# Serial scatters, a later row lookup, router counts one slot on, and another form for the first magnitudes: four small moves in an attention and mixture-of-experts kernel

## The chip, the cores and the metric

The kernel runs on one core of a Trainium2 chip. The metric is the device time of one execution in microseconds (us), lower is better. The engines are PE (TensorE), DVE (VectorE), ACT (ScalarE), POOL (GpSimd) and SP (SyncE, which here only issues DMAs). Each engine takes its instructions in the order of the program; they wait for each other by semaphores. POOL issues the indirect DMAs, that is, scatters and gathers whose row numbers lie in SBUF.

## What is computed

The reference is one transformer layer on x of 8 batches x 1024 tokens x 512 features, in float32. The attention has 16 heads of 32. Its queries, keys and values are cosines and sines, looked up in a table, of the normalised input divided by 1 + |w|; the expert layer sends each token to two of eight experts, 160 places per batch and expert.

```python
x = x + attention(layernorm(x))     # theta_q = xh / (1.0 + jnp.abs(w_q)) + b_q + t * phi_q
...                                 # theta_o = out / (1.0 + jnp.abs(w_out)) + b_out
x = x + ffn(layernorm(x))
...
probs = jax.nn.softmax(x @ Wr + br, axis=-1)
topk_p, topk_e = jax.lax.top_k(probs, K)
pos_all = jnp.cumsum(oh, axis=1) - oh           # oh: one-hot of the chosen experts
keep = pos < cap
h = jax.nn.relu(jnp.einsum('enc,ech->enh', buf, W1) + b1[:, None, :])
y = jnp.einsum('enh,ehc->enc', h, W2) + b2[:, None, :]
```

## The kernel before

The order of the work on PE, ACT, DVE and SP is written out by hand: generators are advanced step by step, and the order in which Python calls them is the order in the queues.

**Start.** Input rows of the first batch are loaded tile by tile (L161). DVE takes statistics of the first two tiles (`first_stats`, L235, L236), prepares 1 / (1 + |w|) for values (`magnitude` and L240 on `rows_in`) and the biases (L242, `wrap`), then the same for queries and keys (`magnitude` and L257 on `inv_qk`), and then the statistics of the other six tiles (L235, L236), the inverse root (L361 to L369), and the normalisation, shared with ACT (L424 to L431). `magnitude` is called a third time for `inv_o` within the first slot. Meanwhile POOL fills constants, clears the value tiles (L377) and computes the position angles (L469), for which it needs `vecs` (L253). Then come transposes (L216), angles and their sines, and the DMAs that put queries and keys into place (L571).

**Attention slots.** A slot n is a batch b and a group c of four heads, n = 4b + c, 32 slots in all. Its two pairs of heads each take `scores` (PE L684 and L698 into a double PSUM bank of `ps_sc`, then ACT's exponential L704, ten tiles) and `attend` (L718, read by DVE L726). While one slot runs, the next one's queries and keys are prepared: `qk_pre` (transposes L216, DVE L525), `angle` (L438), squares, sines, and `qk_post` (DVE L448 and the DMAs L609). `turn` transposes the attention's result. `two_banks()` hands out one of three double banks; transposes, scores, and the router share them.

**Router.** The router of batch b - 1 is a generator advanced within the slots of batch b. In slot c = 1 it computes the logits, in c = 2 the choice of experts (`part`, up to the step named "places"). The next step counts the earlier tokens of each expert:

```python
yield "places"
place = one_bank()[:, : NTT * E]
flat = lambda t: t.rearrange("p t e -> p (t e)")
tokens_out(place, before, flat(mask), start=True, stop=False)
tokens_out(place, ones, flat(prior), start=False, stop=True)
```

`tokens_out` (L858) issues the small matmuls; DVE reads the bank twice (L966, L967), and the step ends at "slots". Before, `route_on(2)` takes this step in slot c = 2, between the first pair's `attend` and the second pair's `scores`. In slot c = 3 the generator ends: slots are computed, and `scatter` issues 16 indirect DMAs (L769) that write token numbers and gates into `slot_d[b]`. Scatters into one `slot_d[b]` wait for each other unless that is declared away; `together=True` declares it away. `late=True` and `together=True` both put the scatter behind POOL's share of the weight mixing (`mixed`, L1213) in POOL's queue. `fetch_slots` (L1005) reads the finished slots back into `meta` when all scatters of the batch have landed.

**Experts.** Weights are mixed by differences (Winograd's form of Strassen: seven products for eight). Each expert has two parts: rows of the first batches (768 rows; three blocks of layer two) and the rest (512 rows). `chunks` lists the 16 parts. Layer one runs over eight groups q (`Hidden`, products L1238, copies and activations on ACT L1248 to L1280, additions on DVE). During the first part's layer one, `ending` is advanced at each product: it finishes the last slot's output and routes the last batch. It ends with `fetch_slots(B - 2)`, the last batch's 16 scatters (`together=True`) and `fetch_slots(B - 1)`. W2 of the first expert (eight DMAs of 512 KB, L1056) is loaded at once, during that layer one.

Layer two of the first part is `layer2`, block by block: products L1352, ACT copies (L1364, L1375, L1377), DVE additions (L1369 to L1400), the gate on ACT (L1311), and an indirect DMA that adds the rows to the output (`send`, L1316). Each of its 21 steps advances `aside` once, which prepares the second part:

- `find_rows(1)` (DVE L1084) turns the slots of the second part into row numbers (`source`); it needs all slots of the last batch. Before, it stands between layer one and layer two.
- `gather(1)`, two steps into layer two (`behind(2, ...)`): four gathers on POOL (L1096), each put out to DRAM (SP L1107) and read back in quarters (SP L1113), a transpose on DVE (L1174) for each, then four additions (L1184 to L1187) that make the operands `xe` and `xe_s` of the second part's layer one.

The mixing of the second part's first weights (`mix_w1`, L1213) is called at the start of the last block.

Of the kernel before, what the change touches and what calls it, by code (L numbers as in the profile page):

```python
# [17 lines left out]
ALU = mybir.AluOpType  # L18
# [8 lines left out]
NTT = S // P  # L27
NCH = D // P
HPC = P // DH
E, HID, TOPK = 8, 2048, 2  # L30
# [30 lines left out]
UNITS = PER_RAD * FINE  # L61
# [13 lines left out]
def preln_attn_moe_kernel(  # L75
# [21 lines left out]
    nc = tc.nc  # L97
# [35 lines left out]
    own = to_router.pool("own", 1, **left)  # L133
# [12 lines left out]
    def token_tiles(dram_rows):  # L146
# [3 lines left out]
    rows_in, spare = (  # L150
        row2.tile([P, D], F32, name="xn2").rearrange("p (i f) -> p i f", f=NCH)[:, :n, :]
        for n in (3, 2)
    )
# [31 lines left out]
    t = xmp.tile([P, NTT, D], F32, name="x_mid").rearrange("p (i t) d -> p i (t d)", i=2)  # L185
    room = [t[:, i, :].rearrange("p (i s) -> p i s", i=2) for i in range(2)]
    for t in (base_first, room[0]):
        nc.gpsimd.iota(
            t, pattern=[[0, 2], [1, S]], base=0, channel_multiplier=0,
# [13 lines left out]
    inv_qk = own.tile([P, 2 * NCH], F32, name="inv_qk")  # L203
# [14 lines left out]
    def magnitude(t):  # L218

        nc.vector.scalar_tensor_tensor(t, t, -1.0, t, ALU.mult, ALU.max)  # L220
        nc.vector.tensor_scalar(t, t, 1.0, None, ALU.add)
        nc.vector.reciprocal(t, t)

    def wrap(t, spare):

        nc.vector.tensor_scalar(spare, t, ROUNDT, ROUNDT, ALU.add, ALU.subtract)
        nc.vector.tensor_tensor(t, t, spare, ALU.subtract)
# [9 lines left out]

    first_stats(0, 2)
    magnitude(rows_in[:, 0, :])
    nc.vector.tensor_scalar(rows_in[:, 0, :], rows_in[:, 0, :], UNITS, None, ALU.mult)  # L240
    b_rows = rows_in[:, 1:, :]
    nc.vector.tensor_scalar(b_rows, b_rows, UNITS, SUM_SHIFT * FINE, ALU.mult, ALU.add)  # L242
    wrap(b_rows, spare)
# [10 lines left out]

    nc.vector.tensor_copy(inv_qk, vecs[:, : 2 * NCH])
    magnitude(inv_qk)
    nc.vector.tensor_scalar(inv_qk, inv_qk, UNITS, None, ALU.mult)  # L257

    ones = own.tile([P, P], F32, name="ones")
    nc.gpsimd.memset(ones, 1.0)  # L260
# [501 lines left out]
    scattered = {b: [] for b in range(B)}  # L762
    mixed = []

    def scatter(count=2 * NTT * TOPK, together=False, late=False):

        for _ in range(min(count, len(scatters))):
            b, idx, src = scatters.pop(0)
            queued = nc.gpsimd.indirect_dma_start(  # L769
                out=slot_d[b], out_offset=bass.IndirectOffsetOnAxis(ap=idx, axis=0),  # L770
                in_=src, in_offset=None,
            )
            ins = queued.ins
            if together or late:
                tc.add_manual_dep(
                    ins, mixed[-1].name,
                    mybir.DependencyInfo(
                        mybir.DependencyClass.NoSync, mybir.DependencyReason.DATA
                    ),
                    reason="behind the mixture",  # L780
                )
            if together:
                for other in scattered[b]:
                    tc.declare_no_dep(ins, other, reason="rows of their own")
            scattered[b].append(ins)

    def router(b):
# [292 lines left out]
    def find_rows(i):  # L1080

        js = slice(chunks[i][1], chunks[i][1] + 2 * chunks[i][2])
        lo, hi = REACH[i]
        nc.vector.tensor_scalar(  # L1084
            source[:, :, js], meta[:, :, js, 0], float(hi * S), float(lo * S),
            ALU.min, ALU.subtract,
        )
# [102 lines left out]
    def behind(count, gen):  # L1190
        for _ in range(count):
            yield
        yield from gen

    def start(gen, box):
        for box[0] in gen:
            yield
# [303 lines left out]
    def seconds(i, hid):  # L1501

        free = places(i, hid)
        if chunks[i][2] == 2:
            rooms = [(free[6 * n : 6 * n + 3], free[6 * n + 3 : 6 * n + 6]) for n in range(2)]
            results = free[12:14]
        else:
            rooms = [(free[:4], free[4:7])] * 2
            results = free[7:9]
        return {w: Second(i, hid, w, *rooms[n % 2]) for n, w in enumerate((5, 2, 3, 4))}, results  # L1510
# [113 lines left out]
    def load_ahead(k):  # L1624
        if k < len(order_):
            load_w1(*order_[k])
# [3 lines left out]
    def experts_begin():  # L1630
# [6 lines left out]
        mix_w1(0, 0)  # L1637

    def experts(ending):
        pools["hp"] = to_end.pool("hp", 1, **right)  # L1640
        pools["ps_tr"] = to_end.pool("ps_tr", 2, space=PSUM, reuse_waits="tile")
        pools["ps_p"] = to_end.pool("ps_p", 6, space=PSUM, reuse_waits="tile")
        box = first_parts
        mixes = loads = iter(())
        for i, (e, j0, nh) in enumerate(chunks):
            parts, box = box[0], [None]
            hid = pools["hp"].tile([P, NHQ, 7, HALF], F32, name="hid")
            tiles, second, early_sums = None, None, iter(())
            if nh == 2:
                second = seconds(i, hid)  # L1650
                early_sums = itertools.chain(second[0][5].weights(), second[0][2].weights())
            ahead = rows_ahead(i + 1) if i and i + 1 < len(chunks) else iter(())
            for q in range(NHQ):
                if i or q != NHQ - AHEAD - 1:
                    load_ahead(i * NHQ + q + AHEAD)
                some(3, loads)
                if q + 1 < NHQ:
                    mix_w1(i, q + 1)
                if i and q > 1:
                    some(4 if q < 4 else 8, mixes)  # L1660
                next(ahead, None)
                if 2 < q < 7:
                    some(2, early_sums)
                beside = [ending] if i or q < NHQ - 2 else [mixes] * (q + 3 - NHQ)
                tiles = layer1(Hidden(i, q, parts, hid, beside), tiles, q == NHQ - 1)
                if i == 0 and q == NHQ // 2:
                    rest(ending)
                    to_router.close()
                    for name, bufs in (("w2p", 1), ("yp", 5), ("bp", 1)):
                        pools[name] = to_end.pool(name, bufs, reuse_waits="tile", **left)  # L1670
                    load_ahead(NHQ - 1)
                    load_b2(0)
                    rest(load_w2(0))
                    mixes = mix_w2(0)
            rest(mixes)
            if i == 0:
                find_rows(1)
            rest(ahead)
            aside = start(gather(i + 1), box) if i + 1 < len(chunks) else iter(())
            if i == 0:  # L1680

                aside = behind(2, aside)

            def mix_next():
                if i + 1 < len(chunks):
                    mix_w1(i + 1, 0)

            if i:
                extra = layer2_quad(
                    i, hid, second, aside, mix_next if nh == 2 else lambda: None  # L1690
                )
                if nh > 2:
                    some(2, aside)
                    for step in range(5):
                        if step == 4:
                            mix_next()
                        next(extra)
                        if step < 2:
                            some(2, aside)
            else:  # L1700
                for block in range(nh):
                    if block == nh - 1:
                        mix_next()
                    for _ in layer2(i, block, hid):
                        next(aside, None)
            rest(aside)
            if i % 2 and e + 1 < E:
                load_b2(e + 1)
                loads = load_w2(e + 1)
                mixes = mix_w2(e + 1)  # L1710
# [22 lines left out]
    begin = False  # L1733
    place, residual = [None], iter(())
    first_gather = gather(0)
    for n in range(NCK):
        more, late = n + 1 < NCK, last is not None
        b, c = divmod(n, NCH)
# [16 lines left out]
        def route_on(slot):  # L1755
            if c == slot and route is not None:
                next(route)
# [15 lines left out]
            turn(0, halves0, pos)  # L1773
        if more:
            angle(*qk_st)
        if begin:
            next(route)
        if n and n + 2 < NCK:
            load_base(n + 2)
# [80 lines left out]
            next(post)  # L1860
        some(NTT, *products)
        route_on(1)
        route_on(2)
        next_pairs = rest(post) if more else None

        es1, halves1 = [[], []], []
# [2 lines left out]
        begin = c == 0 and late  # L1869
# [25 lines left out]
    def ending():  # L1895

        o_st = o_pre(NCK - 1, pos_n)
        scatter(NTT * TOPK // 2, late=True)
        yield
        sine(o_st[1])  # L1900
        square(o_st[0])
        for _ in range(3):
            yield
        for _ in o_post(NCK - 1, o_st):
            yield
        yield
        steps = 0
        for name in router(B - 1):

            if steps in (0, 3):  # L1910
                scatter(NTT * TOPK // 4, late=True)
            steps += 1

            for _ in range({"tiles": 5, "places": 5}.get(name, 1)):
                yield
        fetch_slots(B - 2)
        scatter(together=True)
        fetch_slots(B - 1)

    experts(ending())  # L1920
# [31 lines left out]
```

## Time and profile before

| | us |
|---|---|
| median of 3 executions | 3180.25 (3177.90 to 3182.41) |
| the profiled execution | 3179.05 |
| its span, first to last instruction | 3177.3 |
| PE, DVE, ACT, POOL busy | 3096.0, 2310.1, 1676.5, 420.6 |
| mean granted clock of TensorE | 0.998 |
| start, to the first scores | 0 to 34.66 |
| attention slots | 34.66 to 1255 |
| first part: layer one, layer two | 1255 to 1343.7, to 1417.0 |
| the other 15 parts | 1417 to 3177 |

The profile gives for each instruction its start from the beginning of the span, its duration, its line in the kernel, and the tiles that it writes and reads ("out<-in"). In square brackets stands how long its engine was idle before it, and what ended that ("<-"). The list of waits adds these up: engine and line that waited, whom for, total, times, longest. "issue" means that the engine waited for nothing that the profile shows. The durations of POOL are rough.

### The profile page before, as it was taken

What the parts mean: (1) busy time and instruction counts of PE and PEld (TensorE: products, weight loads), DVE (VectorE), ACT (ScalarE), POOL (GpSimd) and SP (SyncE); (2) the same over time, 40 slices, a digit from 0 to 9 for tenths busy, and PEclk for the clock granted to TensorE, in tenths of its full rate; (3) what the DMA queues carried; (4) which work ended last, traced back from release to release, by engine and by line L of the source; (5) the groups of instructions that cost most, each with busy time, mean ns of one, the idle gap of its engine ahead of it and who ended that gap; (6) DMA issues with size and microseconds to landing.
All of it is one profiled execution on the core that took longest, in us unless ns stands there. A gap on an engine that the chain in (4) does not pass through costs nothing.

```text
span 3177.3 us, 52455 instructions
## 1 busy us (share of the span) xinstructions
PE 3096.0 (97%) x20086; PEld 2147.3 (68%) x20086; DVE 2310.1 (73%) x4808; ACT 1676.5 (53%) x2630; POOL 420.6 (13%) x387
## 2 busy tenths in 40 slices
PE   5999999999999999999999999999999999999998
PEld 2544454444444444589699699699698698698697
DVE  8888888888788776638668658758657667767765
ACT  7888888888788885413423423423423423423423
POOL 3000202020111122410110110110110110110010
PEclk9999999999999999999999999999999999999999
DMA  5435454554545352433523523523533433433421
GB/s 167 147 100 166 125 155 135 148 146 133 164 130 160 81 167 70 134 77 99 156 53 90 153 54 97 146 57 98 141 63 101 132 67 100 129 69 106 119 57 24
DMA packets 288554, 358.80 MB, mean 113 GB/s; under 512 B 28376, under 2 KB 199088, under 8 KB 276272
## 3 DMA queue, kind: packets, MB, share of 16 engines
q1 hardware_dynamic: 264944, 312.20, 33.3%
q0 software_dynamic: 22912, 43.22, 7.3%
q8 instruction: 160, 2.62, 0.4%
q14 instruction: 90, 0.74, 0.1%
q10 hardware_dynamic: 448, 0.02, 0.0%
HBM read 207.02 MB, written 81.22 MB: 91 GB/s over the span
## 4 chain that ended last, share of the span: by engine, by line
PE 78%; ACT 11%; DVE 7%; issue 2%; DMA 2%; SPq 0%; another core or an unknown queue 0%; POOLq 0%; POOL 0%; ACTq 0%; DVEq 0%
PE ps_p L1238 30%; PE ps_p L1474 10%; PE ps_p L1537 10%; PE ps_s L684 9%; PE av L718 9%; PE ps_p L1352 8%; ACT e L704 6%; PE ps_s L216 1%; ACT qk_c L594 1%; DMA xn_d<-xn 1%; ACT t_r L445 1%; ACT qk_r L445 1%; PE ps_s L698 1%; ACT L594 1%; DVE qk_f L525 1%
## 5 line engine op out<-in xcount | busy, mean ns | idle before, releaser
L684 PE MATMUL ps_s<-qk 64*128 64x512 f32 (+3 forms) x3072 | 584.1, 502 | 33.5 <-DMA qk<-qk_r 12.5
L704 ACT ACTIVATE e<-ps_s 128x1024 f32<-128x1024 f32 (+1 forms) x640 | 555.1, 944 | 85.6 <-PE ps_s L698 46.2
L718 PE MATMUL av<-e,v 128*64 128x512 f32 (+3 forms) x3072 | 509.5, 488 | 0.0
L684 PEld LDWEIGHTS ps_s<-qk 64*128 64x128 f32 x3072 | 261.4, 187 | 219.6 <-ACT e L704 93.1
L718 PEld LDWEIGHTS av<-e,v 128*64 128x64 f32 x3072 | 206.0, 137 | 278.8 <-issue 258.6
L1238 PE MATMUL ps_p<-xe,t 128*128 128x256 f32 (+1 forms) x1024 | 317.7, 433 | 2.7 <-ACT hid L1271 2.7
L1238 PE MATMUL ps_p<-xe_s,t 128*128 128x256 f32 (+1 forms) x1024 | 317.8, 433 | 2.3 <-issue 2.3
L1238 PE MATMUL ps_p<-xe,w 128*128 128x256 f32 (+1 forms) x1024 | 317.6, 433 | 0.0
L1316 POOL DMA_INDIRECT out_dram<-y,slots x80 | 127.4, 1593 | 1267.8 <-ACT y L1311 1016.9
L769 POOL DMA_INDIRECT slot_d<-token,slot x128 | 153.8, 1201 | 994.4 <-issue 636.4
L1238 PEld LDWEIGHTS ps_p<-xe_s,t 128*128 128x128 f32 x1024 | 194.3, 190 | 84.0 <-issue 3.7
L1238 PEld LDWEIGHTS ps_p<-xe,t 128*128 128x128 f32 x1024 | 194.2, 190 | 83.4 <-ACT hid L1271 3.3
L1238 PEld LDWEIGHTS ps_p<-xe,w 128*128 128x128 f32 x1024 | 193.7, 190 | 78.2
L1537 PE MATMUL ps_p<-w_t,hid 128*128 128x256 f32 x960 | 212.4, 379 | 0.8 <-DVE y L1590 0.8
L1281 DVE TENSOR_TENSOR hid<-hid 128x256 f32<-128x256 f32 (+1 forms) x128 | 63.0, 492 | 203.7 <-ACT hid L1279 200.9
L1537 PEld LDWEIGHTS ps_p<-w_t,hid 128*128 128x128 f32 x960 | 180.0, 190 | 24.4 <-DVE y L1590 1.2
L1238 PE MATMUL ps_p<-xe_s,w 128*128 128x256 f32 (+1 forms) x512 | 158.9, 433 | 1.1 <-ACT p L1254 1.1
L726 DVE TENSOR_SCALAR av_sb<-av,inv_o 128x512 f32<-128x512 f32 x128 | 94.8, 746 | 70.7 <-PE av L718 70.7
L1352 PE MATMUL ps_p<-w,hid 128*128 128x256 f32 x640 | 142.9, 379 | 0.0
L1474 PE MATMUL ps_p<-w,hid 128*128 128x128 f32 x1104 | 141.8, 275 | 0.0
L1311 ACT ACTIVATE y<-y,slots 128x256 f32<-128x256 f32 (+1 forms) x120 | 65.9, 578 | 142.8 <-DVE y L1389 105.5
L698 PEld LDWEIGHTS <-keys_b 64*128 64x128 bf16 x1536 | 78.9, 95 | 90.7 <-issue 71.9
(291 smaller groups left out, 5229.3 us busy)
## 6 DMA issues: line engine op xcount, KB each, us to landing
w<-in_L_ffn_W_dram SPq DMA_DIRECT2D x256, 256.0 KB
w<-in_L_ffn_W_dram SPq DMA_DIRECT2D x64, 512.0 KB
qk<-qk_c SPq DMA_DIRECT2D x124, 256.0 KB
qk<-qk_r SPq DMA_DIRECT2D x120, 256.0 KB
qk_base<-base_d SPq DMA_DIRECT2D x28, 1024.0 KB
xn_d<-xn SPq DMA_DIRECT2D x72, 256.0 KB
rows_d<-xg SPq DMA_DIRECT2D x70, 256.0 KB
x_mid<-in_L_attn_x_dram SPq DMA_DIRECT2D x16, 1024.0 KB
```

What stands on the lines that cost most here:

```text
L684: nc.tensor.matmul(ps[:, a, at : at + w], lhsT=pair[r, 1, kb * P : (kb + 1) * P], rhs=pair[r, 0, q0 : q0 + w], start=at == 0, stop=not own ...
L698: nc.tensor.matmul(out_, lhsT=keys_b[r, part, :], rhs=late, start=False, stop=part == 1, skip_group_check=True,)
L704: nc.scalar.activation(e, ps[:, :, :n], AF.Exp, scale=UNIT * UNIT / math.sqrt(2 * DH))
L718: nc.tensor.matmul(av[a * 64 : (a + 1) * 64, q0 - 512 * h :], lhsT=vt[:, kb, 2 * pr + a, :], rhs=es[i][:, a, at : at + w], start=kb == 0, ...
L726: nc.vector.tensor_scalar(av_sb, av, inv_o[:, q : q + 1], None, ALU.mult)
L769: queued = nc.gpsimd.indirect_dma_start(out=slot_d[b], out_offset=bass.IndirectOffsetOnAxis(ap=idx, axis=0), in_=src, in_offset=None,)
L1238: nc.tensor.matmul(ps, lhsT=weights[:, k, :], rhs=rows[:, k, :], start=first and k == 0, stop=last and k == 1, skip_group_check=True,)
L1311: nc.scalar.activation(part, part, AF.Identity, scale=meta[:, e, jj[r], 1:2].bitcast(F32))
L1316: ins = nc.gpsimd.indirect_dma_start(out=out, out_offset=bass.IndirectOffsetOnAxis(ap=meta[:, e, jj[r], 0:1], axis=0), in_=y, in_offset=No ...
L1352: nc.tensor.matmul(ps, lhsT=hid[:, k, part, cols], rhs=ws[weight][:, k, :], start=first and k == 0, stop=last and k == NHQ - 1, skip_group ...
L1474: nc.tensor.matmul(ps, lhsT=left[:, k, :], rhs=right[:, k, :], start=first and k == 0, stop=k == 3, skip_group_check=True,)
L1537: nc.tensor.matmul(ps[:, b * DC : (b + 1) * DC], lhsT=hid[:, k, part, b * P : (b + 1) * P], rhs=ws[weight][:, k, :], start=first and k == ...
```

## The change

Four edits; no arithmetic is added or left out, apart from the form of some one-operand instructions.

1. `magnitude` adds its 1 by SCALAR_TENSOR_TENSOR, as max(t + 1, t), where it was a TENSOR_SCALAR; the scaling behind it at two places (`in_units`) likewise, as max(UNITS t, t).
2. The router's counts are no longer taken by `route_on(2)` in slot c = 2, but in slot c = 3, right after `angle`: PE issues them behind the two sets of transposes and ahead of `attend`, and DVE's four instructions stand behind L438. This holds for seven batches; the last batch's router runs in `ending`.
3. The last batch's scatters are issued with `late=True`: each waits for the one before it to land.
4. `find_rows(1)` becomes the ninth step of layer two's `aside`, and `gather(1)` follows it. On DVE the lookup now stands behind the whole of block 0; on POOL the first two sends stand ahead of the four gathers; on DVE the first transpose stands late in block 1, the second at its end, the third and fourth behind the mixing L1213 and ahead of block 2.

```diff
     def magnitude(t):

         nc.vector.scalar_tensor_tensor(t, t, -1.0, t, ALU.mult, ALU.max)
-        nc.vector.tensor_scalar(t, t, 1.0, None, ALU.add)
+        nc.vector.scalar_tensor_tensor(t, t, 1.0, t, ALU.add, ALU.max)
         nc.vector.reciprocal(t, t)
+
+    def in_units(t):
+
+        nc.vector.scalar_tensor_tensor(t, t, UNITS, t, ALU.mult, ALU.max)
...
-    nc.vector.tensor_scalar(rows_in[:, 0, :], rows_in[:, 0, :], UNITS, None, ALU.mult)
+    in_units(rows_in[:, 0, :])
...
-    nc.vector.tensor_scalar(inv_qk, inv_qk, UNITS, None, ALU.mult)
+    in_units(inv_qk)
...
-    def scatter(count=2 * NTT * TOPK, together=False, late=False):
+    def scatter(count=2 * NTT * TOPK, late=False):
...
-            if together or late:
+            if late:
...
-            if together:
-                for other in scattered[b]:
-                    tc.declare_no_dep(ins, other, reason="rows of their own")
...
+    def later_on(do, *args):
+        do(*args)
+        yield
...
-            if i == 0:
-                find_rows(1)
             rest(ahead)
             aside = start(gather(i + 1), box) if i + 1 < len(chunks) else iter(())
             if i == 0:
-                aside = behind(2, aside)
+                aside = itertools.chain(behind(8, later_on(find_rows, 1)), aside)
...
-        if begin:
+        if begin or c == 3 and b > 0:
             next(route)
...
         route_on(1)
-        route_on(2)
         next_pairs = rest(post) if more else None
...
-        scatter(together=True)
+        scatter(late=True)
         fetch_slots(B - 1)
```

## The prediction, made before the result was known

> **What bounds the kernel now.** The page first:
>
> ```profile
> PE 3096.0 (97%) x20086; PEld 2147.3 (68%) x20086; DVE 2310.1 (73%) x4808; ACT 1676.5 (53%) x2630; POOL 420.6 (13%) x387
> ```
>
> TensorE is busy for 97%, so of 3177.3 us only 81 us are its idle time. No edit takes work from it; a gain can only come out of those 81 us. So the second view is the list of PE's waits (total, times, longest):
>
> ```profile
> PE ps_s L216 <- DVE xn L431: 13.5, 1, 13.5
> ...
> PE ps_s L684 <- DVE tmp L966: 5.0, 7, 0.7
> ...
> PE ps_p L1238 <- ACT hid L1271: 2.7, 1, 2.7
> PE ps_p L1238 <- issue: 2.3, 1, 2.3
> ```
>
> 13.5 us lie at the start, where the first transposes wait for DVE; 5.0 us are seven stalls in which scores wait for DVE's reading of the router's counts; 2.7 and 2.3 us lie at 1330 to 1337 us, at the end of the first expert's layer one. These are the three places that the change touches.
>
> **The first magnitudes.** The timeline of DVE at the start (start, duration, line, operation):
>
> ```profile
> 5.54 2.03 DVE L221 TENSOR_SCALAR xn<-xn 128x4 f32<-128x4 f32 x1
> ...
> 8.81 0.17 DVE L220 SCALAR_TENSOR_TENSOR inv_qk<-inv_qk 128x8 f32<-128x8 f32 x1
> 9.02 0.90 DVE L221 TENSOR_SCALAR inv_qk<-inv_qk 128x8 f32<-128x8 f32 x1
> ...
> 10.19 0.97 DVE L257 TENSOR_SCALAR inv_qk<-inv_qk 128x8 f32<-128x8 f32 x1
> ```
>
> The same tiny TENSOR_SCALAR takes 0.17 us at L240 and 2.03, 0.90 and 0.97 us here. POOL's timeline has the memsets of v from 5.62 to 7.45, and L469 from 8.68 to 9.89 and from 9.95 to 11.14: the long ones end within 0.12 us of POOL's. SCALAR_TENSOR_TENSOR at 8.81 lies inside the first L469 and takes 0.17. So in the new form each costs 0.17, and I walk the queue with the starts of the trace (0.20 to 0.24 from one to the next). L221 at 5.54, reciprocal 5.74, L240 5.95, then L242 at 6.15, which stays a TENSOR_SCALAR and is now the one that waits, to 7.57, where L221 ended before. L226 and L227 follow, L253 comes at 7.9 (before: 8.40), L255 8.1, L220 8.3, L221 8.5, reciprocal 8.7, the scaling 8.95, and the memset L282 at 9.15 (before: 11.12). That is **2.0 us**. Is something else late then? The six later tiles of x have landed by 10.5 to 11 us (the DMA's GB/s falls to nothing there), and their statistics would run from 9.4, one each 0.8 us, the last at 13.3: no wait. ACT's roundings (9.93 to 16.7) move by the 0.5 us of L253, to 16.2, and its L427, which now idles 2.10 us for DVE's L424, would find that done at 16.8. The inv_o magnitude (47.3 us) costs 0.17 before and after. From L427 on, transposes, angles and DMAs follow each other; PE's first scores (34.66) come 2.0 us sooner.
>
> **The counts.** Before, eight small matmuls (L858) stand ahead of the second pair's scores:
>
> ```profile
> 280.69 0.32 PE L858 MATMUL ps_s<-mask,before 128*32 128x64 f32 x8
> 281.09 0.32 PE L858 MATMUL ps_s<-prior,ones 128*32 128x64 f32 x8
> 281.34 1.13 PE L684 MATMUL ps_s<-qk 64*128 64x512 f32 x4
> ...
> 285.25 4.56 PE L684 MATMUL ps_s<-qk 64*128 64x512 f32 x20 [0.73 <-DVE tmp L966]
> ...
> 291.33 0.67 PE L216 MATMUL ps_s<-ident,xn 64*128 64x64 f32 x16
> ```
>
> The counts hold one of three double banks until DVE, busy with the 2.28 us product L448, reads them at 284.47. Two banks are left: the third tile waits for the first exponential (it starts at 283.73), the fourth 0.73 us for DVE. From the counts to the next transposes it is 10.64 us, at 584 and 1195 us just so. The next slot has no counts in this place and takes 317.88 to 326.58, 8.70 us. Less the counts' own 0.65, which only moves, the excess is 10.64 - 0.65 - 8.70 = 1.29 us. ACT becomes free (table load, warm-up) 1.38 us after the scores' new start at 280.69, in the next slot 1.28; that costs 0.1. So 1.19 x 7 batches = **8.3 us**. Bounds: 5.0 (the named stalls alone) and 9.0 (7 x 1.29).
>
> In the new place, behind the transposes of the next slot, the counts need the bank of the last exponential: 1.41 + 8.65 = 10.06 us after the scores' start, while PE gets there at 10.2. Their four DVE instructions (4 x 0.26 = 1.03 us) queue behind L438, which ends at 297.76; behind them are av_sb L726 (later by 1.03, but the next av needs its bank only at 309.98) and the statistics; DVE then idles 2.39 us before 300.81, which hides it. The third score tile now waits for this bank: read by 298.8, wanted at 302.82, 4 us of cover. In the old place DVE's L448 of qk_r, and its DMAs on SP behind it, come 0.9 us sooner.
>
> **Scatters and row lookup.** POOL's timeline, and DVE's in layer two:
>
> ```profile
> 1313.70 1.04 POOL L769 DMA_INDIRECT slot_d<-token,slot  x1 [13.22 <-DVE token L982]
> ...
> 1333.42 0.96 POOL L769 DMA_INDIRECT slot_d<-token,slot  x1 [0.30 <-issue]
> ...
> 1354.78 1.01 POOL L1096 DMA_INDIRECT xe_s<-xn_d,source  x1 [13.40 <-ACT y L1375]
> ```
>
> The last 16 scatters are issued 1.3 us apart. One behind another they take: 2.4 us apart where DMA is quiet (1235 to 1242), 7.07 at worst under a full load (1266.39 to 1273.46), 3.48 to 4.04 on average in the six batches of the attention. W2's 4 MB keep the DMA full from 1313.6 to about 1335, then it is quiet until 1358. So three in the first 21 us and twelve gaps of 2.4 after: the last is issued at about 1364 (bounds 1350 and 1374, all at 2.4 or all at 4.04). Landing and the two reads of the slots take 4.8 us more, to 1369. The lookup now stands behind the first block's DVE work, which ends at 1371.4: no wait. But on POOL two sends of the first block (L1316) now stand ahead of the four gathers; the pairs at 1391.99 and 1416.11 show a second send 5.6 us after the first. Sends at 1369 and 1374.6, gathers from 1376.5. Before, the first transposed rows began 14.9 us after the first gather (1354.78 to 1369.72): now 1391.4, and DVE gets to that at 1390.8. Rows are complete 27.4 us after the first gather (1382.15), plus 1.7 for the weight mixing now among them: 1406, wanted at 1417. First to suffer would be ACT's gate behind the first transpose (L1397, L1311), which delays L1364's copy; PE needs that by 1399.6, so the transpose may start 5.3 us later. I take **0**. Bounds: nothing, and with pitch 4.04 a last scatter at 1374 and 4 to 5 us of stall. On the other side are the stalls of 2.7 and 2.3 us: ACT idles 6.0 us ("issue") and 3.7 us ("remote") there, waiting for nothing of the program, and PE waits for it. The scatters lie in that stretch, so a gain of up to 4.9 cannot be excluded. But they take 1 to 7% of the DMA time there, the W loads the rest, and the DMA's bandwidth collapses (55 GB/s at 1327) in the same manner at 1628, 1634 and 1864 under later W2 loads, without scatters. I take nothing.
>
> **Sum.** 2.0 + 8.3 + 0 = 10.3 us. The profiled execution took 3179.05 (span 3177.3), 1.2 under the median of 3180.25; on its own scale that is 3168.8, on the median's **3170**.
>
> **Rivals.**
> Forecast as summed: 3170, chance 0.50.
> (a) The 16 scatters in flight are what starves ACT at 1326 to 1337. For it: nothing else is new there. Against: the shares above. Then 4.9 us more go: 3165; chance 0.15.
> (b) The new form waits for POOL as well, where POOL reads: both edits of inv_qk then end where they ended before, less 0.5, and the start gains 0.5 instead of 2.0: 3171.5. The 0.17 at 8.81, inside L469, speaks against it. The Trainium skill (SBUF — State Buffer, "Who interferes with whom") states just this rule: a DVE instruction with two SBUF inputs contends with a GpSimd instruction that reads SBUF. By that rule the row at 8.81 should have been held to 9.89; the trace disagrees. Chance 0.13.
> (c) The counts bring back in the next slot what they gave up, a DVE late by over 4 us at 298.8. Nothing in the slot shows that; the trouble would take all 8.3: 3178. Chance 0.08.
> (d) Slower: the scatters stay behind the W loads. The stall is about last scatter - 1369.5: first an ACT copy that waits, then rows that come too late for the second part. At a pitch of 4.0 it is 4 us (3174, chance 0.08); from 4.7 on (last at 1384) all is lost, and at 5, last at 1388.7, it is 19: 3189, chance 0.06. For it: one gap of 7.07, and 4.04 as a batch's mean. Against: a quiet DMA from 1337.
>
> A measurement of this kernel tells about 0.2% (6.4 us) from no change. Faster by more: forecast, (a), (b) and half of the 3174, some 0.77 with room for mis-sized terms; within: 0.16; slower: 0.07. Range: from below (a), 3163.5, to above the 3174 of (d), 3176; left out are (c) and the slow end of (d).
>
> **What would show it.** Start: L221 and the scalings at 0.17, one long L242, first L216 at 17.3 instead of 19.27. Counts: the row "DVE tmp" gone from PE's waits, scores of the second pair in 8.8 us. Handover: scatters 2.4 to 7 us apart, gathers about 20 us later than 1354.78 (less the gain so far), no wait of L1352 or of the second part's first L1238 over 1 us, and the two waits of 2.7 and 2.3 still there. The forecast is wrong if PE waits for hid or xe behind layer two, or if the scores of the second pair still take 10 us.

## The result, and the profile after

| | before, us | after, us |
|---|---|---|
| median, measured beside each other (6 runs each) | 3181.2 (3174.89 to 3185.54) | 3166.95 (3164.23 to 3170.23) |
| ratio, 95% interval | | 0.9957 (0.9945 to 0.9970) |
| profiled execution; its span | 3179.05; 3177.3 | 3168.15; 3166.4 |
| first scores | 34.66 | 34.09 |
| first `attend` | 47.45 | 47.82 |
| last transposes of the attention | 1253.79 | 1247.63 |
| layer one, from; how long | 1255.11; 88.58 | 1250.15; 82.62 |
| layer two and on, to the end | 1833.6 | 1833.7 |

The forecast was 3170 and faster. The sum is near; its terms are not. In the page of after PE's busy time is 3093.3 (3096.0 before), so 2.7 of the 10.9 us of span are work of PE that took less time and 8.2 are idle time:

```profile
PE 3093.3 (98%) x20086; PEld 2146.6 (68%) x20086; DVE 2307.3 (73%) x4808; ACT 1676.1 (53%) x2630; POOL 424.4 (13%) x387
```

The list of PE's waits (total, times, longest). First a row of before that stands beside the four shown in the prediction, then after:

```profile
PE ps_s L684 <- ACT e L704: 7.6, 10, 3.7
```

```profile
PE ps_s L216 <- DVE xn L435: 12.9, 1, 12.9
PE ps_s L688 <- ACT e L708: 12.7, 15, 3.7
...
PE ps_p L1243 <- issue: 1.1, 1, 1.1
```

The start's wait fell by 0.6, not by 2.0. The row for `tmp` is gone, but the scores' wait for ACT's exponentials, 7.6 us in ten waits before, is now 12.7 in fifteen. And the 2.3 and 2.7 us at the end of layer one, which the forecast left standing, are gone; in their place PE waits 1.1 us at layer one's start.

**Start.** DVE in after, then POOL beside it (start, duration, line):

```profile
5.87 1.70 DVE L246 TENSOR_SCALAR xn<-xn 128x8 f32<-128x8 f32 x1
...
8.31 0.17 DVE L220 SCALAR_TENSOR_TENSOR inv_qk<-inv_qk 128x8 f32<-128x8 f32 x1
8.51 0.89 DVE L221 SCALAR_TENSOR_TENSOR inv_qk<-inv_qk 128x8 f32<-128x8 f32 x1
...
9.67 0.97 DVE L226 SCALAR_TENSOR_TENSOR inv_qk<-inv_qk 128x8 f32<-128x8 f32 x1
10.62 0.17 DVE L286 MEMSET vec_in<- 128x128 f32 x1
```

```profile
8.18 1.21 POOL L473 TENSOR_SCALAR qk_base<-qk_base,vecs 128x1024 f32<-128x1024 f32 x1 [0.64 <-DVE vecs L257]
...
9.44 1.19 POOL L473 TENSOR_SCALAR qk_base<-qk_base,vecs 128x1024 f32<-128x1024 f32 x1
```

In the new form the two edits of `inv_qk` take 0.89 and 0.97, as long as in the old one, and end with POOL's L473. Only the first `magnitude`, beside POOL's memsets, became short.

**Counts.** PE in the second batch, slots c = 2 and c = 3:

```profile
282.46 1.13 PE L688 MATMUL ps_s<-qk 64*128 64x512 f32 x4
...
291.17 0.67 PE L216 MATMUL ps_s<-ident,xn 64*128 64x64 f32 x16
...
292.63 0.32 PE L859 MATMUL ps_s<-mask,before 128*32 128x64 f32 x8
292.76 0.29 PE L859 MATMUL ps_s<-prior,ones 128*32 128x64 f32 x8
292.99 7.96 PE L722 MATMUL av<-e,v 128*64 128x512 f32 x48
...
304.62 4.61 PE L688 MATMUL ps_s<-qk 64*128 64x512 f32 x20 [0.93 <-ACT e L708]
```

The scores of c = 2 take 8.71 us, as forecast, and the counts cost 0.36 in their new place. But the slot after has a wait of 0.93 that before has not. Its origin, followed back through ACT, DVE and SP's DMA queue:

```profile
299.58 2.19 ACT L446 ACTIVATE qk_f<-qk_f,split_c 128x1024 f32<-128x1024 uint16 x2 [4.40 <-DVE qk_r L442]
...
303.57 8.45 ACT L708 ACTIVATE e<-ps_s 128x1024 f32<-128x1024 f32 x10
```

```profile
298.32 1.23 DVE L442 TENSOR_SCALAR qk_r<-qk_f 128x2048 int32<-128x2048 int32 x1 [1.84 <-DMA qk<-qk_r]
```

```profile
289.07 4.12 SPq L613 DMA_DIRECT2D qk<-qk_r  x4
```

`angle` (L442, L438 before) writes the tile `qk_r`, which the last slot's DMAs must first have emptied. Counted from the `attend` ahead (272.80 before, 274.57 after), L438 began at 23.73 and L442 at 23.75: it did not move. Before had the same wait, 0.88 us long, and it cost PE nothing there:

```profile
296.53 1.23 DVE L438 TENSOR_SCALAR qk_r<-qk_f 128x2048 int32<-128x2048 int32 x1 [0.88 <-DMA qk<-qk_r]
```

```profile
302.00 8.65 ACT L704 ACTIVATE e<-ps_s 128x1024 f32<-128x1024 f32 x10
```

The `attend` of slot c = 3 moved from 20.00 to 18.42. ACT's squares wait for L442 and stand ahead of the exponentials (L704, L708 after); these now begin 2.69 us behind the scores' start, where it was 1.31, and PE waits.

The places at which `attend` begins give the whole account. In each of seven batches slot c = 3 comes sooner by 1.34 to 1.58 us, 10.8 in all; the next `attend` gives back 1.19, 1.23, 0.17, 1.38, 1.63, 0.64 and 0, 6.2 in all. So 4.6 us stay.

**Handover.** POOL in after:

```profile
1356.09 0.96 POOL L773 DMA_INDIRECT slot_d<-token,slot  x1 [1.42 <-DMA slot_d<-token,slot]
1358.48 1.58 POOL L1006 DMA_DIRECT2D slots<-slot_d  x2 [1.44 <-DMA slot_d<-token,slot]
1360.36 1.68 POOL L1321 DMA_INDIRECT out_dram<-y,slots  x1 [0.30 <-issue]
...
1367.98 1.01 POOL L1097 DMA_INDIRECT xe_s<-xn_d,source  x1 [0.30 <-issue]
```

Scatters lie 2.4 to 6.8 us apart. From layer two's start to the last scatter, the first gather and the complete rows it is 23.3, 35.2 and 59.7 us (forecast 20.3, 32.8, 62.3), and no wait of PE over 0.5 us follows.

### The profile page after: what moved, and what is told of

Same layout as the page of the kernel before. It is cut to its first block, busy times and chain, and to the rows that moved or that the text cites. A ratio compares the mean times of both kernels' runs of the same rounds, so it can differ in the third digit from the quotient of the medians.

```text
span 3166.4 us, 52470 instructions
## 1 busy us (share of the span) xinstructions
PE 3093.3 (98%) x20086; PEld 2146.6 (68%) x20086; DVE 2307.3 (73%) x4808; ACT 1676.1 (53%) x2630; POOL 424.4 (13%) x387
## 4 chain that ended last, share of the span: by engine, by line
PE 75%; ACT 13%; DVE 6%; issue 3%; DMA 2%; SPq 0%; ACTq 0%; POOLq 0%; POOL 0%; DVEq 0%
PE ps_p L1243 30%; PE ps_p L1479 10%; PE ps_p L1542 10%; PE ps_p L1357 8%; PE ps_s L688 7%; PE av L722 7%; ACT e L708 7%; ACT qk_c L598 1%; PE ps_s L216 1%; ACT t_r L449 1%; ACT qk_r L449 1%; DMA xn_d<-xn 1%; ACT L598 1%; DVE qk_f L529 1%; ACT L1857 1%
## 5 line engine op out<-in xcount | busy, mean ns | idle before, releaser
L688 PE MATMUL ps_s<-qk 64*128 64x512 f32 (+3 forms) x3072 | 584.4, 503 | 31.8 <-ACT e L708 12.7
L708 ACT ACTIVATE e<-ps_s 128x1024 f32<-128x1024 f32 (+1 forms) x640 | 554.3, 943 | 71.4 <-PE ps_s L702 43.8
L1479 PEld LDWEIGHTS ps_p<-w,hid 128*128 128x128 f32 x1104 | 135.8, 192 | 2.3
```

The lines of the kernel that those rows point to most:

```text
L688: nc.tensor.matmul(ps[:, a, at : at + w], lhsT=pair[r, 1, kb * P : (kb + 1) * P], rhs=pair[r, 0, q0 : q0 + w], start=at == 0, stop=not own ...
L708: nc.scalar.activation(e, ps[:, :, :n], AF.Exp, scale=UNIT * UNIT / math.sqrt(2 * DH))
L1479: nc.tensor.matmul(ps, lhsT=left[:, k, :], rhs=right[:, k, :], start=first and k == 0, stop=k == 3, skip_group_check=True,)
```

## The experiments

Before and after were run again beside the experiments, in three further measurements; before took 3170.74, 3171.23 and 3170.76 there (medians of 19 to 26 runs), 10 us less than in the first. These three ran on three different chips; which chip the first ran on is not on record. All ratios are to the before of the same measurement. "Last attend" is the start of the last `attend`, at 1245.89 in the first profile of before and 1239.74 in that of after.

| kernel | median, us | ratio (95%) | last attend | layer one | clock lost by 1260 |
|---|---|---|---|---|---|
| counts alone | 3166.30 | 0.9989 (0.9979 to 0.9998) | 1235.24 | 82.62 | 1.7 |
| lookup alone | 3171.08 | 1.0001 (0.9992 to 1.0011) | 1243.44 | 83.20 | 3.4 |
| serial scatters alone | 3186.74 | 1.0047 (1.0030 to 1.0064) | 1244.30 | 82.67 | 3.4 |
| after, halves swapped | 3157.15 | 0.9956 (0.9939 to 0.9972) | 1230.72 | 82.61 | 3.4 |
| before again | 3171.89 | 1.0000 (0.9990 to 1.0010) | 1246.83 | 82.84 | 6.8 |
| after again | 3166.28 | 0.9987 (0.9977 to 0.9996) | 1237.41 | 82.62 | 5.1 |
| after, PSUM magnitudes | 3166.72 | 0.9984 (0.9974 to 0.9993) | 1237.18 | 83.79 | 6.8 |
| after, both | 3159.78 | 0.9959 (0.9945 to 0.9973) | 1231.15 | 82.62 | 5.1 |
| before, a third time (1 run) | 3166.11 | | 1238.25 | 83.03 | 0.0 |
| both handover edits alone | 3168.48 | 0.9993 (0.9983 to 1.0003) | 1237.89 | 83.10 | 0.0 |
| before, halves swapped | 3167.60 | 0.9989 (0.9979 to 0.9998) | 1243.81 | 82.67 | 6.8 |
| both, PE kept busy | 3164.42 | 0.9984 (0.9974 to 0.9993) | 1235.24 | 83.46 | 1.7 |

The last column adds up, over windows of 1 us, what the granted clock is below 1; it is explained under the last experiment. In the first pair it is 3.4 (before) and 5.1 (after). In two rows, 83.79 and 83.46, one such loss lies within layer one and makes it longer.

**Counts alone.**

```diff
-        if begin:
+        if begin or c == 3 and b > 0:
             next(route)
...
         route_on(1)
-        route_on(2)
```

> The kernel before with the router's counts moved to slot c = 3, and nothing else. Theory A (the wait moves on): in the profile after, the second pair's scores of slot c = 2 take 8.71 us, and with the counts behind them the attention comes 1.58 us sooner per batch; but in the next slot DVE's L438 still waits for the DMA that empties qk_r, ACT's squares and exponentials follow it, and PE waits for ACT, so 1.0 us of 1.58 is given back on average. So about 4 to 5 us are gained by the end of the attention, PE's list has more waits for ACT's e (12.7 us where before has 7.6), and none for tmp. Rival B (the give-back is chance or comes from another edit): 7 x 1.58 = 11 us by the end of the attention. As nothing is changed in the scatters, the two waits of PE at the end of layer one (2.3 and 2.7 us) should stand here as before; if they are gone, they hang on chance and not on the scatters. Whole kernel: A 3176, B 3170.

Theory A holds: the seven gains are there (1.57 or 1.58, the last 1.34), and 0.69, 1.17, 1.18, 1.45, 1.17, 0.85 and 0 are given back. The median is 4.4 us less. The last `attend` alone would speak for rival B, for it is 10.65 us sooner than in the first profile of before. But only 4.3 of that lie in the slots c = 3 and behind them; 3.0 lie in one router's slot at 815 us and the rest in other slots whose times differ between executions. Against before a third time, the last `attend` is 3.0 sooner. PE's list in this kernel:

```profile
PE ps_s L684 <- ACT e L704: 12.8, 17, 3.7
...
PE ps_p L1238 <- issue: 1.1, 1, 1.1
```

The 1.1 at layer one's start comes with the counts: all seven kernels with moved counts show it there, none of the seven others does. From the last `attend` to layer one it is 10.4 us with it and 9.2 without, a further 1.2 off the gain. PE waits there for nothing that the profile shows ("issue"); why is open. The two waits at the end of layer one are absent, though this kernel's last 16 scatters are in flight together.

**Lookup alone.**

```diff
-            if i == 0:
-                find_rows(1)
...
-                aside = behind(2, aside)
+                aside = itertools.chain(behind(8, later_on(find_rows, 1)), aside)
```

> The kernel before with only the row lookup moved into layer two; the last 16 scatters stay in flight together. Theory A (scatters in flight starve ACT): ACT idles 6 and 3.7 us at the end of layer one as before, PE waits some 5 us there, and layer one lasts 88.6 us (1255.1 to 1343.7 before; 82.6 after). Rival B (the lookup's place or chance): the waits are gone, layer one lasts 83 to 84 us. Whole kernel: A within 1 us of before, B 5 us less.

Rival B: layer one takes 83.2 us with all scatters in flight, and the time is that of before. The edit is worth nothing by itself. That the time is not 5 us less, as B had it, fits a before without the stall: no profile of before was taken in this measurement, but its median, 3170.74, is that of the two others, whose profiles of before have none (below).

**Serial scatters alone.**

```diff
-        scatter(together=True)
+        scatter(late=True)
```

> The kernel before with only the last scatters one behind another; the lookup stays between layer one and layer two. Theory A: the waits of 2.3 and 2.7 us in layer one are gone, layer one lasts 83 to 84 us. Then DVE waits in the lookup for the last scatter: in the profile after, slots are complete 29 us after layer two's start (1362 against 1332.8), and DVE's additions of layer two stand behind it; PE has six banks, about 10 us of work, so some 15 to 20 us are lost there and the kernel takes 3190 to 3197. Rival B (the waits have nothing to do with scatters in flight): both, 3195 to 3202, with layer one at 88.6 us.

The lookup waits 20.3 us on DVE for the last scatter, and PE behind DVE, first in DVE's timeline, then in PE's list:

```profile
1366.65 0.18 DVE L1084 TENSOR_SCALAR source<-slots 128x32 int32<-128x32 int32 x1 [20.32 <-DMA slots<-slot_d]
```

```profile
PE ps_p L1352 <- DVE y L1395: 11.6, 1, 11.6
...
PE ps_p L1352 <- ACT y L1364: 3.1, 1, 3.1
```

Layer two takes 92.97 us instead of 73.30. The waits are 14.7 us of these 19.7. Between 1359 and 1391 us the granted clock is 0.5 for 20.5 us; PE worked for 10.8 of these at half its clock, which is worth 5.4 us and covers the other 5. So the later lookup is what makes the serial scatters possible; neither gains by itself.

**Halves swapped.** On after: ACT takes the sine of `qk_r` first, DVE its product, SP its DMAs.

```diff
-        nc.scalar.activation(c, c, AF.Sin, bias=quarter_c, scale=-STEP_ACT)
-        for _ in between:
-            pass
         sine(r)
+        nc.scalar.activation(c, c, AF.Sin, bias=quarter_c, scale=-STEP_ACT)
...
-        for i, t in enumerate((st[0], st[2].bitcast(F32))):
+        for i, t in ((1, st[2].bitcast(F32)), (0, st[0])):
```

> The changed kernel, with the two halves of the queries' and keys' angles in the other order everywhere: ACT takes the sine of qk_r ahead of that of qk_c, DVE forms the product of qk_r first, and its DMAs go out first. Theory A (in slot c = 3 the exponentials wait for squares, these for DVE's L442, and L442 for the DMA that empties qk_r, 1.84 us in the second batch): the DMA of qk_r goes out 2.9 us sooner, DVE waits there no longer, and the 6.2 us that six batches give back come in: the attention ends 5 to 6 us sooner than after, 3161 to 3162 in all. Rival B (the DMAs together are late, whatever their order): now ACT's L589, which writes qk_c, waits for the DMA of qk_c, and no more than 1 us is gained. Rival C: PE's exponentials in the slots are late for another reason, and nothing changes.

Theory A. DVE's L442 no longer waits (the row has no brackets), ACT's squares begin at 295.63 instead of 299.58, and PE's list is back at the 7.6 us in ten waits of before:

```profile
294.38 1.22 DVE L442 TENSOR_SCALAR qk_r<-qk_f 128x2048 int32<-128x2048 int32 x1
```

```profile
PE ps_s L688 <- ACT e L708: 7.6, 10, 3.7
```

All seven gains stay (1.34 to 1.58), and what is given back is within 0.01 us in each batch. The kernel takes 3157.15, 4 us less than was expected; the next control bears on that.

**Before, halves swapped.** The same edit on before.

> The kernel before with the halves of the angles in the other order, the counts left in slot c = 2. If the swap gained by taking away the wait which the moved counts had made (theory A), there is nothing to take here: before's slots c = 3 have no such wait, the time stays within 2 us of before. If the swap is a gain by itself (rival B), 6 us less than before, as between the changed kernel with and without it.

The `attend` of the slots c = 3 do not move against before, so nothing was to be had there: theory A for the wait. But the median is 3.2 us less (interval 0.6 to 6.7). Between two profiles that lost equally much clock, this one and before again, the last `attend` is 3.0 us sooner, nearly all of it in the router's slots. Those slots differ as much without the swap: in the six profiles with the attention of before, the seven slots c = 1, less the lost clock, add up to 289 to 293 us, and here to 290. So the profiles do not show that the swap gains by itself. Of its gain in the changed kernel (9 us between the medians here and of after again, which are of different measurements; 6.5 for the version with both edits against after, in one measurement), 6 us are those that were given back, and the rest is not placed.

**Before, again and a third time; after again.** No edit.

> The kernel before once more, for a second profile on another day or chip. Theory A (the waits of 2.3 and 2.7 us at the end of layer one belong to the kernel before, with or without scatters): layer one lasts 88.6 us as in the first profile. Theory B (they belong to some chips or executions only, as two kernels with the same 16 scatters in flight had none and took 82.6 and 83.2 us): 82 to 84 us. The time is that of before, ratio 1.000.

> The kernel before a third time, for its profile on whichever chip this is. Layer one took 88.58 us in the first profile and 82.84 in the second. If the time is near 3180 and layer one near 88, the stall of ACT comes with some chips; if it is near 3171 and 83, this run tells nothing new of it.

> The changed kernel once more, beside before on the same chip. If the 4.9 us at the end of layer one came from that one chip's state, the change is worth here what its attention is worth, 4 to 6 us (ratio 0.998 to 0.9988); if the scatters do it, 10 to 14 us (0.9957 to 0.997). Layer one lasts 82.6 us by both.

The stall at the end of layer one is in one profile of before out of three. Layer one takes 82.84 and 83.03 us in the others, and 83.20 in the kernel with the lookup alone, all with the 16 scatters in flight. Where before lacks the stall, the change is worth 5.0 us, 0.9987 (0.9977 to 0.9996). The counts alone are worth 4.4 and the handover alone 2.3, the latter with no change within its interval. In the first measurement it was worth 14.25, and all six runs of before took 3174.9 or more, so the stall, 6.0 us in the profiled execution, may well lie in all of them; the other 4 us by which before was slower there have no profile to explain them. What caused it there is open: after, with serial scatters, lacks a stall that before, with parallel ones, had in that one measurement, and five profiles elsewhere (before again and a third time, the counts alone, the lookup alone, before with swapped halves) show parallel ones without it. That it belongs to one chip is neither shown nor excluded.

**Both handover edits alone.** The diffs of the two experiments above together, on before.

> The kernel before with both edits of the handover, serial scatters and the later lookup, and nothing else. Layer one 82.6 us, no wait of PE behind layer two (in the changed kernel there was none over 0.5 us). On a chip where before takes 3171, theory A (the handover's edits are worth nothing by themselves, the stall was of one chip) expects the same time as before within 0.1%; rival B (serial scatters are worth 5 us) 3166. On a chip where before takes 3180: 5 us or more below it if the scatters in flight cause the stall, the same if not.

No wait of PE behind layer two, layer two 73.30 us. The ratio, 0.9993 (0.9983 to 1.0003), holds theory A's 1.000 and, at its edge, B's 0.9985. The profiles decide: this kernel and before a third time both lost no clock by 1260, and their layer one lasts 83.10 and 83.03 us, their spans 3163.8 and 3164.4. So A: the forecast's 0 for the handover holds where before has no stall.

**Magnitudes in PSUM.** On after:

```diff
-    nc.vector.tensor_copy(inv_qk, vecs[:, : 2 * NCH])
-    magnitude(inv_qk)
-    in_units(inv_qk)
+    q = ps[:, : 2 * NCH]
+    nc.vector.scalar_tensor_tensor(q, q, -1.0, vecs[:, : 2 * NCH], ALU.mult, ALU.max)
+    nc.vector.tensor_scalar(q, q, 1.0, None, ALU.add)
+    nc.vector.reciprocal(q, q)
+    nc.vector.tensor_scalar(inv_qk, q, UNITS, None, ALU.mult)
```

> The changed kernel, with the magnitudes of queries and keys formed in PSUM: four DVE instructions that read at most one SBUF operand (the first) or none, and a copy less. Theory A (an instruction that reads SBUF twice waits while POOL's L473 reads SBUF, one that works in PSUM does not): each takes about 0.2 us where L221 and L226 took 0.89 and 0.97, the memset L286 comes at about 9.1 instead of 10.62, and the first scores 1.5 us sooner, at 32.6. Rival B (any DVE instruction waits there): 0.9 and 1.0 as before. As for the end: the first scores came 0.5 us sooner in the changed kernel and in the one with swapped halves, yet attend began 0.37 later and 0.10 sooner than before, where kernels without the form had -0.11 to +0.16; so the first scores' slow rows (0.8 us for 512 columns where it is 0.28 later) may absorb all of it: then attend begins at 47.3 as ever. If they do not, at 45.9.

```profile
8.11 0.17 DVE L260 SCALAR_TENSOR_TENSOR ps_s<-ps_s,vecs 128x8 f32<-128x8 f32 x1
8.32 0.17 DVE L261 TENSOR_SCALAR ps_s<-ps_s 128x8 f32<-128x8 f32 x1
8.53 0.22 DVE L262 RECIPROCAL ps_s<-ps_s 128x8 f32<-128x8 f32 x1
8.78 0.17 DVE L263 TENSOR_SCALAR inv_qk<-ps_s 128x8 f32<-128x8 f32 x1
9.01 0.17 DVE L288 MEMSET vec_in<- 128x128 f32 x1
```

Theory A: with POOL's instruction at 8.18 as ever, none of them waits, and the memset comes 1.6 us sooner. The first transposes come at 17.79 (18.79 in after again): 0.6 of it is lost to small DVE instructions behind the statistics, which now meet other work of POOL (0.33 and 0.37 for two that took 0.20 and 0.17). The first scores begin at 33.09, the first `attend` at 46.85. In the eight kernels with the old form that one lies between 47.34 and 48.22, in the three with the new form between 47.35 and 47.82: the 0.5 us that the form gave the first scores is lost in that scatter. With the PSUM form it is 46.85 here, and 46.85 and 46.31 in the two kernels below that have it too: 0.5 to 1.0 sooner than the earliest of the others, where the first scores are 1.0 to 1.5 sooner. The whole time tells neither (0.9984 beside 0.9987).

**Both.** The swapped halves and the magnitudes in PSUM, on after.

> The changed kernel with both edits, magnitudes in PSUM and the halves of the angles in the other order. It should be faster than after by what the swap alone gives, 6 to 9 us, and by 0 to 1.5 us at the start; 3155 to 3157 where before takes 3170.7.

3159.78, 0.9959 (0.9945 to 0.9973): as with the swap alone. These two are the fastest versions.

**PE kept busy.** On the last version, in the first slot, where PE waits 3.7 us for ACT:

```diff
         some(3, *ahead)
+        if n == 0:
+            unused = ps_av.tile([P, 512], F32, name="av")
+            for _ in range(20):
+                nc.tensor.matmul(
+                    unused[:64, :], lhsT=v_tiles[0][:, 0, 0, :], rhs=es[0][0][:, 0, :],
+                    start=True, stop=True,
+                )
```

> The changed kernel with magnitudes in PSUM, the swapped halves, and 20 matmuls of 512 columns whose result nobody reads, where PE waits 3.7 us for ACT's exponentials in the first slot (58 to 62 us). They add work to PE and nothing to the output. If the fall of the granted clock to 0.5 behind this wait (4 to 8 us long in every profile so far, 1.7 to 3.7 us of clock lost) follows from PE's pause, it is gone, and the second attend begins 1.7 to 3 us sooner against the first attend: the distance is 23.7 us in the first profile of before and up to 24.8 in others, here 22 to 23. If the clock falls for another reason, it falls still, or the 20 matmuls (3.3 us) only push the scores back. Whole kernel: 2 us less than the one without them, 3157 to 3158, or the same.

My size was wrong: the 20 matmuls take 17.4 us, not 3.3 (the trace has each as two rows, of 0.43 us). So 13.7 us of them lie beyond the wait, and the kernel is slower than without them (0.9984 where it was 0.9959). The clock stays whole in the first slots, the wait being filled. But it also stays whole in two kernels with the wait, so this one run does not show that the wait was the cause; the same window of two profiles of before does show what the fall costs. Before again, then before a third time (window, length, busy times of PE, PEld, DVE, ACT, POOL, then the granted clock, DMA share, GB/s):

```profile
62.00:66.00 4.00, 3.37 (x8) 1.79 (x10) 3.97 (x4) 3.01 (x4) 0.00 (x0) 0.50 1.04 248
```

```profile
62.00:66.00 4.00, 3.64 (x18) 1.72 (x20) 3.93 (x5) 4.00 (x6) 0.00 (x0) 1.00 1.03 236
```

The same kernel, the same 3.70 us of waiting just ahead: once 8 matmuls fall into 62 to 66 us, once 18. Before again loses 6.8 us of clock by the end of the attention, the third profile none, and their last `attend` lie 8.6 us apart. While its clock was halved PE worked long enough for 5.5 us of these.

## Why the forecast came near, point by point

- **Start, 2.0 us: wrong.** The step that failed is "So in the new form each costs 0.17". It rested on L220 at 8.81, which took 0.17 "inside" L469. In after L220 again begins 0.13 us behind POOL's instruction and takes 0.17, and L221, 0.20 later, takes 0.89. So the first tenths of POOL's row do not hold DVE back, and the row at 8.81 was no witness. This was rival (b), with its size: 0.5 on DVE, 0.57 at the first scores, nothing that can be told at the first `attend`. The Trainium skill (SBUF — State Buffer, "Who interferes with whom") had the rule that a DVE instruction with two SBUF inputs contends with a GpSimd instruction that reads SBUF. I had said that the trace disagreed; with 0.89 and 0.97 here, and 0.17 to 0.22 in PSUM, the runs agree with that rule, all but L220, which begins 0.13 us behind POOL's row and is not held in either profile.
- **Counts, 8.3 us: the mechanism right, the size of one term off, and one term missing.** Each batch gives 1.57 where I took 1.19: the window is 8.71 as forecast, but the counts cost 0.36 in the new place, not the 0.65 that I left in, and ACT's 0.1 did not show. That would be 10.8. The missing term is the DMA that empties `qk_r`: I had looked at the bank in slot c = 3 (4 us of cover, which held) and at the place of the product of `qk_r` on DVE (0.9 us sooner, which held as well), but not at when its DMA lands, which stayed where it was while PE came 1.58 sooner. That L438 already waited 0.88 us for this DMA in before was the sign that it had no time to spare. 6.2 us go there, as the swap shows by getting them back, and 1.2 at layer one's start. Rival (c) had the place, the next slot, and the wrong mechanism and price.
- **Handover, 0: right by itself.** The steps came within 3 us (last scatter, gathers, complete rows), the cover held, and the two edits alone are worth 0.9993 with no change in the interval. Rival (d) needed a mean pitch of 4.7 us; it was 3.2 to 3.4.
- **"ACT stalls of 2.7 and 2.3 us still there": wrong in the first pair.** Layer one took 6.0 us less, the size of rival (a). The experiments do not bear out (a)'s cause: five profiles with all scatters in flight have no stall. A stall of one profile was counted as part of the kernel.
- **Sum.** 0.57 instead of 2.0; 4.6 less 1.2 instead of 8.3; 6.0 instead of 0. The remaining 1 us is the first slot (2.0 us back, half of it clock) against 3.0 us won in the router's slots. The sum of 10.9 is near 10.3 by luck: the stall, which the forecast had left standing, paid for what the other two terms lacked. Without it, in the measurement with before and after again, the change is worth 5.0 us.

## What to carry to other kernels

Where a wait of one engine is taken away, ask not only whether the instructions of the next slot are in time but when its buffers come free: a DMA that reads a tile late does not move up with the engine, and the next writer of that tile hands the time back. Take a gap for the kernel's own only when a second profile has it too. A row that overlaps another by its first tenths is no proof that the two do not contend.

## What the runs showed of the hardware

- The granted clock falls to 0.5 within or just behind short pauses of PE, in one execution and not in another: at the wait of 3.70 us in the first slot in 11 of 13 profiles, and in 9 of 14 in one router's slot (the fall begins at 827.8 to 837.7 us), where in the first profile of before three waits of 1.0, 0.8 and 1.0 us follow each other. What is lost by 1260 us is 0, 1.7, 3.4, 5.1 or 6.8 us, that is, the clock is halved for 3.41 or 6.83 us at a time (13.65 at the wait of 11.6 us with serial scatters alone). The Trainium skill (TensorE: Matmul & The Clock Gate, "What's actually happening") describes a free-running window of 3413 ns; the multiples agree with it. That an idle window is needed, as it says, does not fit the falls behind waits of 1 us with matmuls between.
- Three profiles of one kernel have spans of 3164.4, 3172.7 and 3177.3 us. Of the 8.3 us between the first two, lost clock while PE worked is 5.5. Of the 12.9 between the first and the third, lost clock is 3.4 and the longer layer one 5.6. Either difference is more than the change is worth by itself.
- A DVE instruction of 8 elements takes 0.17 us alone and up to 0.97 beside a POOL instruction that reads SBUF; beside POOL's memsets a TENSOR_SCALAR waits (L246, 1.70) and a SCALAR_TENSOR_TENSOR of 4 elements does not (L226, 0.16, begun 0.16 behind a memset of 0.94), though so early a start is, by the first point above, weak evidence.
